# Position scores through memory in three transfers per tile, and the fourth tile's products earlier: one change to the last stage of a perceiver layer

## The chip, the core and the metric

The kernel runs on one core of a Trainium2 chip. The metric is the device time of one execution in microseconds (us), the median of several runs. The kernel before takes 3286.47 us (three runs, 3283.05 to 3294.87).

## The reference

Two layers work on x, 8 batches of 64 tokens with 512 features. The first has a cross attention over a context of 1601 rows, a Fourier attention and an expert layer. The second has a cross attention, a self attention with relative positions, and a quantized feed-forward layer. Only the last two blocks matter here:

```python
# _L1_attn_ref: 16 heads of 32, S = 64
r = _sinusoid_rel_pos(S, dk)
term1 = einsum('bhqd,bhkd->bhqk', Q, K)
term2 = einsum('bhqd,kd->bhqk', Q, r)
term3 = einsum('hd,bhkd->bhk', u, K)[:, :, None, :]
term4 = einsum('hd,kd->hk', v, r)[None, :, None, :]
scores = (term1 + term3 + _rel_shift(term2 + term4)) / sqrt(dk)
out = einsum('bhqk,bhkd->bqhd', softmax(scores), V).reshape(B, S, H * dv) @ Wo + bo
```

`_rel_shift` puts a column of zeros ahead of the 64 columns of each row, reads the 64 x 65 numbers as 65 x 64, and drops the first 64. The feed-forward layer rounds its weights to -1, 0 and 1 and its activations to 8 bits, and applies a gelu between its two products.

## The kernel before

`l1_tail` (from L1633) computes these two blocks. The 512 tokens are four tiles of 128, each with two batches (b). Tiles 0 to 2 form the group `first` and tile 3 the group `last`, because tile 3's x is completed last by the cross attention ahead of this stage. TensorE (PE) does the products, VectorE (DVE) and ScalarE (ACT) take results out of PSUM and do the softmax, GpSimd (POOL) adds biases, raises to the power of minus a half and clears borders, and SyncE (SP) issues all transfers, in the order in which they are written.

For a group, `turn` (L1694) transposes the normalized x into `xT`, `queries` (L1709) multiplies by Wq and makes two copies of the result for each tile: `qu` (with u added, by VectorE, L1722) and `qv` (with v added, by ScalarE, L1717). `of_pairs` (L1728) multiplies such a copy with a right side, per chunk c of 128 features, batch b and half j: 16 products of 64 rows by 64 columns in two passes each, into two PSUM banks. It serves the position scores (right side r, `y_ps`) and the scores (right side the keys, `s_ps`).

`positions_of` (L1747) does the relative shift. It copies the position scores of a tile into `y` (two buffers) with a zero column in front of each row, 65 numbers per row, and writes them to `shift[t]` in memory, in four transfers (two batches b, two heads h of a pair). `shifted` (L1770) reads them back one row (64 numbers) later, as rows of 64, into `z[t]` (three buffers), again in four transfers; a read can only be issued when its write has landed. A row of 65 numbers is a segment of 260 B and a row of 64 one of 256 B: per tile 2048 of each.

Each transfer uses one of eight semaphores in turn, and waits on SP until the transfer eight before it has landed. The order on SP is: Wq and small constants, Wk, Wv, Wo, the writes of tiles 0, 1 and 2 (12), the reads of tiles 0, 1 and 2 (12), `bo`, w1 (4), w2 (4), `b1`, `b2`, then the four writes and four reads of tile 3 and the four outputs.

Then come `keys` (kT, L1796), `values` (v, and x plus `bo` on GpSimd, L1806), and for each tile `probabilities` (L1808: s_ps plus z into `p`, then maximum, difference, exp, sum, reciprocal and product, L1815 to L1824), `turn` (transposes of p, L1833, copies by ScalarE, L1834), `attend` (o_ps, L1846, two halves weighted into `oT`, L1855 and L1856) and `out` (times Wo, L1864, added to x, L1871). `hidden` (L1883) normalizes and rounds a row, transposes it (`levels_ps`, L1877), multiplies by w1 (`h_ps`, L1902), adds b1 (L1906) and applies gelu and squares (L1907, L1909); `hidden_levels` rounds again, and `layer2` transposes the result, multiplies by w2 (L1930) and writes the output.

PSUM is held in three pools: `pe` (three banks, tag "e": y_ps, q_ps, xt_ps, h_ps), `pm` (three banks, tag "mm": k_ps, s_ps, v_ps, pT_ps, o_ps, out_ps) and `pt` (two banks: levels_ps).

The program is written in the order of the last lines of `l1_tail`, and a scheduler then orders the instructions of each engine; each engine works through its own queue in that order. In the built program VectorE's two copies of `v_ps` stand ahead of `p` of tile 0, and PE's queue has, after the scores of tile 0, the v products, the transposes and q products of tile 3 between them, then pT, o and out of tile 0, the scores of tile 1, the rest of q and y of tile 3, pT and o of tile 1, the levels of tile 0, out of tile 1, k and v of tile 3, the h products of tile 0 and the scores of tile 2.

Of the kernel before, what the change touches and what calls it, by code (L numbers as in the profile page):

```python
# [10 lines left out]
F32 = mybir.dt.float32  # L11
# [8 lines left out]
P = 128  # L20
B, S, D = 8, 64, 512
NT = B * S // P
DC = D // P
# [928 lines left out]
class Experts:  # L952
# [22 lines left out]
    def load(self, e):  # L975
        if e >= E_:
            return
        nc, d = self.K.nc, self.d
        w1, w2 = [], []
        for n in range(4):  # L980
            t = self.place(4 * e + n, "w1")
            nc.sync.dma_start(t, d["L0f_W1"][e, :, ts(n, 512)].rearrange("(c p) n -> p c n", p=P))
            w1.append(t)
        for n in range(4):
            t = self.pool.tile([P, DC, 512], F32, tag="w2", name="w2")
            nc.sync.dma_start(t, d["L0f_W2"][e, ts(n, 512), :].rearrange("(c p) n -> p c n", p=P))
            w2.append(t)
        self.held[e] = w1, w2
# [565 lines left out]
class TernaryWeights:  # L1554
# [46 lines left out]
        nc.vector.tensor_scalar(q, q, 1.0, -1.0, ALU.min, ALU.max)  # L1601
        nc.sync.dma_start(self.to[i], self.shaped(q, i))

    def load(self, pool):
        nc = self.nc
        self.w1 = pool.tile([P, DC, HID], BF16, tag="w1q", name="w1q")
        self.w2 = pool.tile([P, HID // P, D], BF16, tag="w2q", name="w2q")
        for c in range(4):
            nc.sync.dma_start(self.w1[:, c, :], self.w1_out[:, c, :])
        for c in range(4):  # L1610
            nc.sync.dma_start(self.w2[:, ts(c, 4), :], self.w2_out[:, ts(c, 4), :])


def rms_levels(K, pool, y, top, mean_square):
# [18 lines left out]
def l1_tail(K, x, d, w, known):  # L1633
# [6 lines left out]
    tc, nc = K.tc, K.nc  # L1640
    FIRST = NT - 1
    with ExitStack() as es:
        ep = es.enter_context(tc.tile_pool(name="e_e", bufs=1))
        wp = es.enter_context(tc.tile_pool(name="e_w", bufs=1))
        rp = es.enter_context(tc.tile_pool(name="e_r", bufs=2))
        dp = es.enter_context(tc.tile_pool(name="e_d", bufs=1, space=DRAM))
        pe = es.enter_context(tc.tile_pool(name="e_pse", bufs=3, space=PSUM))
        pm = es.enter_context(tc.tile_pool(name="e_psm", bufs=3, space=PSUM))
        pt = es.enter_context(tc.tile_pool(name="e_pst", bufs=2, space=PSUM))

        def big(name):
            return ep.tile([P, HID], F32, tag="big", name=name, bufs=3)
# [22 lines left out]
        uv = weight(ep, "L1a_uv", [P, 2, DC], d["L1a_uv"])  # L1675
        own = weight(ep, "c_own", [P, 4], d["c_own"])
        rT = weight(ep, "c_rT", [P, S], d["c_rT"])
        shift = [
            dp.tile([2, 2, DC, 2, S * (S + 1)], F32, tag=f"shift{t}", name="shift") for t in range(NT)
        ]  # L1680
        vs = ep.tile([P, DC, 2], F32, tag="vs", name="vs")
        for s in range(2):
            nc.vector.tensor_scalar_mul(vs[:, :, s], uv[:, 1, :], own[:, s : s + 1])
# [1 line left out]
        class Group:  # L1685
# [61 lines left out]
        def positions_of(t, qv):  # L1747
            y = ep.tile([P, 2, DC, 2, S + 1], F32, tag="y", name="y", bufs=2)
            halves = of_pairs(pe, "e", qv, lambda r, c, b: rT[r], "y_ps")
            nc.gpsimd.memset(y[:, :, :, :, 0:1], 0.0)  # L1750
            for j in range(2):
                K.copy(y[:, j, :, :, 1:], halves[j])
            for b in range(2):
                for h in range(2):
                    nc.sync.dma_start(
                        shift[t][b, :, :, h, :].rearrange("j c (q k) -> q (j c) k", k=S + 1),
                        y[ds(64 * h, 64), :, :, b, :].rearrange("q j c k -> q (j c) k"),
                    )

        first = Group(ep, list(range(FIRST)))  # L1760
        first.turn()
        first.queries()
        for t in first.tiles:
            positions_of(t, first.qv[t])
        wk = chunked(big("L1a_Wk"), "L1a_Wk")
        wv = chunked(big("L1a_Wv"), "L1a_Wv")

        z = {}

        def shifted(t):  # L1770
            z[t] = wp.tile([P, 2, 2, DC, S], F32, tag="z", name="z", bufs=3)
            for b in range(2):
                for h in range(2):
                    nc.sync.dma_start(
                        z[t][ds(64 * h, 64), b].rearrange("q j c k -> q (j c) k"),
                        shift[t][b, :, :, h, S:].rearrange("j c (q k) -> q (j c) k", k=S),
                    )

        for t in range(FIRST):
            shifted(t)  # L1780
        wo = chunked(wp.tile([P, HID], F32, tag="L1a_Wo", name="L1a_Wo"), "L1a_Wo")
        bo = weight(wp, "L1a_bo", [P, D], bcast_rows(d["L1a_bo"]))
        w.load(wp)
        b1 = weight(wp, "b1", [P, HID], bcast_rows(d["L1f_b1"]))
        b2 = weight(wp, "b2", [P, D], bcast_rows(d["L1f_b2"]))

        groups = [first]
        kT = wp.tile([P, DC, B * S], F32, tag="kT", name="kT")
        v = wp.tile([P, NT, D], F32, tag="v", name="v")

        def keys(g):
            n = len(g.tiles) * P
            for c in range(DC):
                ps = pm.tile([P, D], F32, tag="mm", name="k_ps")[:, :n]
                g.project(wk, c, ps)
                nc.scalar.copy(kT[:, c, ds(g.tiles[0] * P, n)], ps)  # L1796

        def values(g):
            for i, t in enumerate(g.tiles):
                ps = pm.tile([P, D], F32, tag="mm", name="v_ps")  # L1800
                for c in range(DC):
                    nc.tensor.matmul(
                        ps, lhsT=g.xT[:, c, ts(i, P)], rhs=wv[:, c, :], start=c == 0, stop=c == DC - 1
                    )
                K.copy(v[:, t, :], ps)
                nc.gpsimd.tensor_add(x[:, t, :], x[:, t, :], bo)  # L1806

        def probabilities(t):  # L1808

            zt = z[t].rearrange("p b j c k -> p j c b k")  # L1810
            p = ring("j", "p")
            qu = groups[t // FIRST].qu[:, :, t % FIRST]
            halves = of_pairs(pm, "mm", qu, lambda r, c, b: kT[r, c, ds((2 * t + b) * S, S)], "s_ps")
            for j in range(2):
                nc.vector.tensor_add(p[:, j], halves[j], zt[:, j])  # L1815
            rows = p.rearrange("p j c b k -> p (j c b) k")
            m = rp.tile([P, 16], F32, tag="m", name="m")
            wide = m.unsqueeze(2).to_broadcast([P, 16, S])
            nc.vector.tensor_reduce(m, rows, AX.X, ALU.max)
            nc.vector.tensor_sub(rows, rows, wide)  # L1820
            nc.scalar.activation(rows, rows, AF.Exp)
            nc.vector.tensor_reduce(m, rows, AX.X, ALU.add)
            nc.vector.reciprocal(m, m)
            nc.vector.tensor_mul(rows, rows, wide)  # L1824
            return p
# [35 lines left out]
        def out(t, oT):  # L1861
            ps = pm.tile([P, D], F32, tag="mm", name="out_ps")
            for c in range(DC):
                nc.tensor.matmul(  # L1864
                    ps,
                    lhsT=oT[:, c].rearrange("p b q -> p (b q)"),
                    rhs=wo[:, c, :],
                    start=c == 0,
                    stop=c == DC - 1,
                )  # L1870
            nc.vector.tensor_add(x[:, t, :], x[:, t, :], ps)  # L1871
# [60 lines left out]
            nc.vector.scalar_tensor_tensor(o, ps, level, x[:, t, :], ALU.mult, ALU.add)  # L1932
            nc.sync.dma_start(d["out"][ts(t, P), :], o)

        keys(first)
        p = probabilities(0)
        values(first)
        out(0, attend(0, turn(p)))
        p = probabilities(1)
        last = Group(wp, [FIRST])  # L1940
        last.turn()
        last.queries()
        positions_of(FIRST, last.qv[0])
        groups.append(last)
        out(1, attend(1, turn(p)))
        keys(last)
        values(last)
        shifted(FIRST)
        got = None
        for t in range(NT):  # L1950
            h = hidden(t)
            if got:
                layer2(t - 1, *got)
            if t + 2 < NT:
                p = probabilities(t + 2)
            got = hidden_levels(*h)
            if t + 2 < NT:
                out(t + 2, attend(t + 2, turn(p)))
# [118 lines left out]
```

## Time and profile before

| what | us or share |
|---|---|
| median of three runs | 3286.47 |
| the profiled execution, as a whole | 3286.85 |
| its span, from the first instruction to the last | 3285.1 |
| PE, DVE, ACT, POOL busy | 97%, 53%, 26%, 31% |
| first y_ps product of this stage | 3111.4 |
| scores of tile 0 done (PE) | 3134.46 |
| p of tile 0 begins (DVE) | 3147.60 |
| pT of tiles 0, 1 and 2 begins (PE) | 3155.33, 3179.16, 3213.32 |

The page of a profile shows one execution. Its slices cut the span into 40 equal parts, a digit being the busy share in tenths. The chain of work that ended last is followed back from the last instruction, at each step to what released it. A table by stage gives the busy time of each engine in stretches of the span, with the granted TensorE clock (1.00 is full, 0.50 half) and the mean busy share of the 16 DMA engines; groups that run into a stretch can make the share more than 1. In the timeline a line gives the start, the length, the engine, the source line, what is written from what, the count, and in brackets the idle time ahead of it with what ended it.

### The profile page before, as it was taken

The numbers are of one execution on the slowest core, as the hardware profiler recorded it, in microseconds if no ns is written. First come the engines' busy times: TensorE is split into PE (matmuls) and PEld (weight loads), VectorE is DVE, ScalarE is ACT, GpSimd is POOL, SyncE is SP. The second block draws the span as 40 slices with busy tenths as digits, with TensorE's granted clock in tenths as the row PEclk, the third lists the DMA queues.
The fourth block names the chain that finished last, engine by engine and source line by source line (L and its number), as shares of the span: only waits on it lengthen the run. The fifth ranks groups of instructions, "written<-read, shape, count | busy, mean of one in ns | idle before, by whom it ended". The sixth has DMA issues, their size and how long they took to land.

```text
span 3285.1 us, 40503 instructions
## 1 busy us (share of the span) xinstructions
PE 3174.3 (97%) x15881; PEld 2162.1 (66%) x15881; DVE 1749.7 (53%) x2929; ACT 846.4 (26%) x1572; POOL 1008.8 (31%) x980
## 2 busy tenths in 40 slices
PE   8999999999999999998899998999999999999986
PEld 6777778888878888885454444555565555655653
DVE  4745565666566656654332234644546455454736
ACT  2222232222233212211012221323233232323323
POOL 5433335444454435430000034123141321403010
PEclk9999999999999999998899998999999999999988
DMA  7254553333355333326278530100101001000250
GB/s 234 77 167 141 162 174 93 105 105 111 108 180 170 103 117 96 105 93 218 72 284 297 200 126 10 31 31 10 41 1 40 20 22 40 1 31 1 60 115 13
DMA packets 314322, 329.03 MB, mean 100 GB/s; under 512 B 35525, under 2 KB 235717, under 8 KB 312981
## 3 DMA queue, kind: packets, MB, share of 16 engines
q1 hardware_dynamic: 310416, 314.88, 30.6%
q10 hardware_dynamic: 3717, 11.57, 0.9%
q8 instruction: 126, 2.06, 0.3%
q14 instruction: 63, 0.52, 0.0%
HBM read 303.30 MB, written 23.10 MB: 99 GB/s over the span
## 4 chain that ended last, share of the span: by engine, by line
PE 89%; DVE 4%; DMA 3%; ACT 1%; issue 1%; POOL 1%; ACTq 0%; SPq 0%; POOLq 0%; DVEq 0%
PE k_ps L1298 11%; PE v_ps L1397 11%; PE x_ps L566 10%; PE x_ps L451 9%; PE z_ps L566 5%; PE s_ps L1411 4%; PE z_ps L451 4%; PE h_ps L1118 3%; PE oe_ps L1145 3%; PE acc L1461 3%; PE y_ps L566 2%; PE y_ps L451 2%; PE sum_ps L1320 2%; PE s_ps L444 1%; DMA w_out<-wq 1%; PE v_ps L599 1%
## 5 line engine op out<-in xcount | busy, mean ns | idle before, releaser
L1335 POOL TENSOR_TENSOR r<-r,minus_half 128x24 f32<-128x24 f32 x64 | 288.7, 4515 | 690.5 <-DVE r L1331 690.5
L1397 PE MATMUL v_ps<-L1x_WvT,ctxT 128*128 128x512 f32 (+1 forms) x832 | 380.2, 605 | 0.0
L1298 PE MATMUL k_ps<-ctxT,L1x_WkT 128*128 128x384 f32 (+1 forms) x1024 | 375.0, 509 | 0.6 <-ACT o L51 0.6
L451 PE MATMUL x_ps<-qt,ctxT 128*128 128x256 f32 x1152 | 286.6, 382 | 5.8 <-DVE s L416 3.8
L566 PE MATMUL x_ps<-pt,ctx 128*128 128x256 f32 x1152 | 280.3, 381 | 1.7 <-ACT u L514 1.0
L1298 PEld LDWEIGHTS k_ps<-ctxT,L1x_WkT 128*128 128x128 f32 x1024 | 183.9, 189 | 140.2 <-issue 42.8
L1397 PEld LDWEIGHTS v_ps<-L1x_WvT,ctxT 128*128 128x128 f32 (+1 forms) x832 | 149.6, 187 | 170.5 <-issue 165.1
L451 PEld LDWEIGHTS x_ps<-qt,ctxT 128*128 128x128 f32 x1152 | 217.2, 190 | 46.2 <-DVE s L416 7.3
L566 PEld LDWEIGHTS x_ps<-pt,ctx 128*128 128x128 f32 x1152 | 216.5, 189 | 35.3 <-DVE a L541 1.6
L122 POOL TENSOR_TENSOR ctxT<-ctxT 128x256 f32<-128x256 f32 x96 | 78.9, 822 | 405.8 <-DMA ctxT<-in_ctxT 355.6
L1411 PEld LDWEIGHTS s_ps<-qb,kT 64*128 64x128 f32 x1664 | 144.3, 187 | 75.4 <-DVE s L1423 44.5
L432 DVE TENSOR_TENSOR m<-m,s 128x512 f32<-128x512 f32 x176 | 131.3, 746 | 94.5 <-ACT s L430 91.8
L1411 PE MATMUL s_ps<-qb,kT 64*128 64x128 f32 x1664 | 171.5, 288 | 7.1 <-DVE s L1423 6.7
L122 POOL TENSOR_TENSOR ctx<-ctx 128x256 f32<-128x256 f32 x96 | 72.2, 752 | 341.4 <-DMA ctx<-in_ctx 276.8
L1302 ACT ACTIVATE kT<-k_ps,L1x_bk 128x384 f32<-128x384 f32 (+1 forms) x128 | 75.9, 593 | 349.5 <-PE k_ps L1298 344.1
L1331 DVE TENSOR_SCALAR r<-sumT_ps 128x12 f32<-128x12 f32 (+1 forms) x128 | 16.5, 166 | 254.5 <-PE sumT_ps L1328 254.1
L1400 ACT COPY v<-v_ps 128x512 f32<-128x512 f32 (+1 forms) x104 | 60.5, 582 | 336.8 <-PE v_ps L1397 336.8
L1423 DVE TENSOR_TENSOR s<-s_ps,r 128x512 f32<-128x512 f32 x192 | 124.6, 683 | 34.4 <-PE s_ps L1411 34.1
L484 DVE TENSOR_TENSOR s<-s,top_ps 128x1024 f32<-128x1024 f32 (+1 forms) x112 | 123.3, 1137 | 20.7 <-PE top_ps L474 20.7
L1452 DVE TENSOR_TENSOR s<-s,top_ps 128x1664 f32<-128x1664 f32 x64 | 117.9, 1884 | 27.1 <-PE top_ps L1448 27.1
L1431 DVE TENSOR_TENSOR fold<-s 128x1536 f32<-128x1536 f32 x64 | 112.1, 1751 | 37.7 <-ACT s L1453 37.7
L416 DVE SCALAR_TENSOR_TENSOR s<-y_ps,bias,p 128x256 f32<-128x256 f32 x96 | 46.3, 483 | 142.8 <-PE y_ps L451 142.7
(405 smaller groups left out, 5776.0 us busy)
## 6 DMA issues: line engine op xcount, KB each, us to landing
w<-in_L0f_W SPq DMA_DIRECT2D x64, 1024.0 KB, 5.4
ctxT<-in_ctxT SPq DMA_DIRECT2D x192, 256.0 KB, 4.4
ctx<-in_ctx SPq DMA_DIRECT2D x192, 256.0 KB, 3.2
ctxT<-in_ctxT SPq DMA_DIRECT2D x24, 768.0 KB, 4.4
wvT<-in_L0x_WvT SPq DMA_DIRECT2D x16, 1024.0 KB, 6.8
qk<-qk_all SPq DMA_DIRECT2D x15, 1024.0 KB, 7.1
qk_all<-stage SPq DMA_DIRECT2D x32, 384.0 KB, 3.5
wraw<-in_L1f_w1T SPq DMA_DIRECT2D x16, 512.0 KB, 4.2
```

Of the source, the lines that this page charges most:

```text
L122: nc.gpsimd.tensor_add(q[:, 4, :], q[:, 2, :], q[:, 3, :])
L432: nc.vector.tensor_max(self.m, self.m if k else self.s[:, LAST, :], self.s[:, k, :])
L451: nc.tensor.matmul(ps, lhsT=ctxT[i][:, Quarters.LEFT[n], ts(e, P)], rhs=right[n][:, e, :], start=start and e == 0, stop=e == 1, skip_group ...
L484: nc.vector.tensor_sub(s[:, k : k + n], s[:, k : k + n], top.unsqueeze(1).to_broadcast([P, n, HALF]))
L566: nc.tensor.matmul(ps, lhsT=ctx[pair][:, Quarters.LEFT[n], ts(m, P)], rhs=right[n][:, i, :], start=start and i == 0, stop=i == 2, skip_gro ...
L1298: nc.tensor.matmul(ps[:, :n], lhsT=wk[:, e, ts(c, P)], rhs=ctxT[i][:, e, :n], start=e == 0, stop=e == DC - 1)
L1335: nc.gpsimd.tensor_tensor(r[:, at : at + n, :], r[:, at : at + n, :], minus_half[:, :n, :], ALU.pow)
L1397: nc.tensor.matmul(ps[:kn], lhsT=ctxT[i][:, c, ds(at, kn)], rhs=wv[:, c, :], start=c == 0, stop=c == DC - 1)
L1411: nc.tensor.matmul(pair[j][:, i, :], lhsT=kT[c][rows, ts(k0 + i, P)], rhs=qb[rows, c, b].rearrange("p h q -> p (h q)"), start=True, stop=True,
L1423: nc.vector.tensor_mul(out, in_, by)
L1431: nc.vector.tensor_tensor(t, s[:, :, 0:6, :], s[:, :, 6:12, :], op)
L1452: nc.vector.tensor_sub(s[:, j], s[:, j], ps[:, j, :].unsqueeze(1).to_broadcast([P, NK, P]))
```

## The change

A tile's position scores now go to memory in one transfer from all 128 partitions, and come back in two (one for each half of 64 partitions), since `y`, `shift` and `z` have the two batches next to each other in memory. The transfers are put in another order on SP: write 0, `bo`, write 1, read 0, write 2, w1, read 1, `b1`, read 2, w2, `b2`. `load` is cut into `load1` and `load2` for that. `keys` and `values` of tile 3 use the banks "e" in place of "mm" and are written before its `positions_of`; `attend` and `out` of tile 1 move behind `hidden(0)`. Lines of the changed kernel are up to four lower than those quoted here.

```diff
-    def load(self, pool):
+    def load1(self, pool):
+    def load2(self, pool):
...
-        shift = [
-            dp.tile([2, 2, DC, 2, S * (S + 1)], F32, tag=f"shift{t}", name="shift") for t in range(NT)
-        ]
+        shift = [dp.tile([16, P * (S + 1)], F32, tag=f"shift{t}", name="shift") for t in range(NT)]
...
-            for b in range(2):
-                for h in range(2):
-                    nc.sync.dma_start(
-                        shift[t][b, :, :, h, :].rearrange("j c (q k) -> q (j c) k", k=S + 1),
-                        y[ds(64 * h, 64), :, :, b, :].rearrange("q j c k -> q (j c) k"),
-                    )
+            nc.sync.dma_start(
+                shift[t].rearrange("g (p k) -> p g k", k=S + 1), y.rearrange("p j c b k -> p (j c b) k")
+            )
...
-        for t in first.tiles:
-            positions_of(t, first.qv[t])
+        def shifted(t):
+            z[t] = wp.tile([P, 2, DC, 2, S], F32, tag="z", name="z", bufs=3)
+            for h in range(2):
+                nc.sync.dma_start(
+                    z[t][ds(64 * h, 64)].rearrange("q j c b k -> q (j c b) k"),
+                    shift[t][:, ds(h * S * (S + 1) + S, S * S)].rearrange("g (q k) -> q g k", k=S),
+                )
+
+        positions_of(0, first.qv[0])
         wk = chunked(big("L1a_Wk"), "L1a_Wk")
         wv = chunked(big("L1a_Wv"), "L1a_Wv")
...
-        for t in range(FIRST):
-            shifted(t)
         wo = chunked(wp.tile([P, HID], F32, tag="L1a_Wo", name="L1a_Wo"), "L1a_Wo")
         bo = weight(wp, "L1a_bo", [P, D], bcast_rows(d["L1a_bo"]))
-        w.load(wp)
+        positions_of(1, first.qv[1])
+        shifted(0)
+        positions_of(2, first.qv[2])
+        w.load1(wp)
+        shifted(1)
         b1 = weight(wp, "b1", [P, HID], bcast_rows(d["L1f_b1"]))
+        shifted(2)
+        w.load2(wp)
         b2 = weight(wp, "b2", [P, D], bcast_rows(d["L1f_b2"]))
...
-        keys(first)
+        keys(first, pm, "mm")
         p = probabilities(0)
-        values(first)
+        values(first, pm, "mm")
         out(0, attend(0, turn(p)))
         p = probabilities(1)
         last = Group(wp, [FIRST])
         last.turn()
         last.queries()
+        keys(last, pe, "e")
+        values(last, pe, "e")
         positions_of(FIRST, last.qv[0])
         groups.append(last)
-        out(1, attend(1, turn(p)))
-        keys(last)
-        values(last)
-        shifted(FIRST)
         got = None
         for t in range(NT):
             h = hidden(t)
-            if got:
+            if t == 0:
+                out(1, attend(1, turn(p)))
+                shifted(FIRST)
+            else:
                 layer2(t - 1, *got)
```

More of the change, by code (lines that the diff above doesn't have):

```diff
@@ L1602, in round @@
         nc.sync.dma_start(self.to[i], self.shaped(q, i))
-    def load(self, pool):
-        nc = self.nc
+    def load1(self, pool):
         self.w1 = pool.tile([P, DC, HID], BF16, tag="w1q", name="w1q")
+        for c in range(4):
+            self.nc.sync.dma_start(self.w1[:, c, :], self.w1_out[:, c, :])
+    def load2(self, pool):
         self.w2 = pool.tile([P, HID // P, D], BF16, tag="w2q", name="w2q")
         for c in range(4):
-            nc.sync.dma_start(self.w1[:, c, :], self.w1_out[:, c, :])
-        for c in range(4):
-            nc.sync.dma_start(self.w2[:, ts(c, 4), :], self.w2_out[:, ts(c, 4), :])
+            self.nc.sync.dma_start(self.w2[:, ts(c, 4), :], self.w2_out[:, ts(c, 4), :])
 def rms_levels(K, pool, y, top, mean_square):
@@ L1762, in l1_tail @@
         first.queries()
-        for t in first.tiles:
-            positions_of(t, first.qv[t])
+        z = {}
+        def shifted(t):
[6 more added lines that the diff above has]
+        positions_of(0, first.qv[0])
         wk = chunked(big("L1a_Wk"), "L1a_Wk")
         wv = chunked(big("L1a_Wv"), "L1a_Wv")
[L1768 to L1777, printed above, removed]
-        for t in range(FIRST):
-            shifted(t)
         wo = chunked(wp.tile([P, HID], F32, tag="L1a_Wo", name="L1a_Wo"), "L1a_Wo")
         bo = weight(wp, "L1a_bo", [P, D], bcast_rows(d["L1a_bo"]))
-        w.load(wp)
+        positions_of(1, first.qv[1])
[3 more added lines that the diff above has]
+        shifted(1)
         b1 = weight(wp, "b1", [P, HID], bcast_rows(d["L1f_b1"]))
+        shifted(2)
+        w.load2(wp)
         b2 = weight(wp, "b2", [P, D], bcast_rows(d["L1f_b2"]))
@@ L1789, in l1_tail, with keys, values @@
         v = wp.tile([P, NT, D], F32, tag="v", name="v")
-        def keys(g):
+        def keys(g, psum, tag):
             n = len(g.tiles) * P
             for c in range(DC):
-                ps = pm.tile([P, D], F32, tag="mm", name="k_ps")[:, :n]
+                ps = psum.tile([P, D], F32, tag=tag, name="k_ps")[:, :n]
                 g.project(wk, c, ps)
                 nc.scalar.copy(kT[:, c, ds(g.tiles[0] * P, n)], ps)
-        def values(g):
+        def values(g, psum, tag):
             for i, t in enumerate(g.tiles):
-                ps = pm.tile([P, D], F32, tag="mm", name="v_ps")
+                ps = psum.tile([P, D], F32, tag=tag, name="v_ps")
                 for c in range(DC):
@@ L1808, in probabilities @@
         def probabilities(t):
-            zt = z[t].rearrange("p b j c k -> p j c b k")
             p = ring("j", "p")
@@ L1814, in probabilities @@
             for j in range(2):
-                nc.vector.tensor_add(p[:, j], halves[j], zt[:, j])
+                nc.vector.tensor_add(p[:, j], halves[j], z[t][:, j])
             rows = p.rearrange("p j c b k -> p (j c b) k")
```

## The prediction

> **What bounds the kernel now.** I read the page first, for the whole program. TensorE (PE) is busy 97% of the span, and its row of slices shows dips only around 1480 to 1640 us, ahead of the experts, and at the end. The diff touches nothing ahead of `l1_tail`, whose products begin at 3111 us of 3285, so 174 us are in question.
>
> ```profile
> PE 3174.3 (97%) x15881; PEld 2162.1 (66%) x15881; DVE 1749.7 (53%) x2929; ACT 846.4 (26%) x1572; POOL 1008.8 (31%) x980
> PE   8999999999999999998899998999999999999986
> ```
>
> Second, the table by stage (stretch and its length, then busy us of PE, PEld, DVE, ACT and POOL, granted clock, DMA share, GB/s), cut where the granted clock changes:
>
> ```profile
> 3113.30:3116.70 3.40, 3.40 (x45) 3.40 (x43) 1.92 (x4) 1.12 (x2) 0.56 (x1) 1.00 0.97 324
> 3116.70:3123.50 6.80, 6.80 (x29) 5.44 (x29) 0.00 (x0) 0.05 (x1) 0.00 (x0) 0.50 1.36 118
> 3123.50:3147.40 23.90, 23.55 (x102) 13.45 (x101) 1.79 (x3) 3.58 (x7) 2.33 (x4) 1.00 1.00 155
> 3147.40:3150.80 3.40, 1.34 (x12) 1.15 (x11) 3.33 (x5) 0.00 (x0) 2.87 (x3) 1.00 1.03 392
> 3150.80:3164.50 13.70, 7.64 (x44) 4.94 (x45) 4.16 (x6) 5.16 (x11) 0.00 (x0) 0.50 0.57 221
> 3171.30:3185.00 13.70, 12.97 (x84) 11.17 (x84) 10.12 (x25) 4.56 (x9) 1.78 (x2) 0.50 0.26 40
> 3202.00:3205.40 3.40, 0.00 (x0) 0.00 (x0) 3.40 (x9) 2.21 (x5) 0.00 (x0) 1.00 0.00 0
> 3205.40:3215.70 10.30, 3.70 (x18) 2.84 (x19) 7.29 (x21) 2.89 (x4) 1.10 (x2) 0.50 0.00 2
> ```
>
> Until 3147 PE is full; then it stands still twice (3147 to 3155, 3202 to 3212), and behind each gap the clock is half. Third, the chain of work that ended last, from start, us, what:
>
> ```profile
> 3134.46 3.64 PE v_ps L1802 x8
> ...
> 3143.47 3.50 PE v_ps L1802 x8
> 3146.97 0.02 issue
> 3146.99 0.04 DVE v L49
> ...
> 3147.60 1.29 DVE p L1815 x2
> ...
> 3155.33 1.98 PE pT_ps L1833 x8
> ...
> 3161.42 5.21 PE out_ps L1864 x8
> 3166.63 1.98 PE s_ps L1738 x32
> ```
>
> The scores of tile 0 (`s_ps`) are done at 3134.46, but VectorE takes them up at 3147.60: its in-order queue has the copies of `v_ps` ahead of that softmax, and these wait for PE. When PE has run out of products the softmax takes 7.73 us with nothing beside it. Fourth, why it was queued so late, from the timeline (start, us):
>
> ```profile
> 3114.21 16.86 SPq L1755 DMA_DIRECT2D shift<-y  x12
> 3131.12 9.89 SPq L1774 DMA_DIRECT2D z<-shift  x12
> 3123.64 0.13 POOL L1750 MEMSET y<- 128x16 f32 x1 [9.59 <-DMA shift<-y]
> ```
>
> All twelve writes go ahead of the first read-back; z of tile 0 is complete at 3139 (fourth read issued 3133.2, 6 us to land).
>
> **The change, part by part.** The built order of the changed kernel is: k, s(0), the three v without a break, turn p(0), attend(0), out(0), s(1), then q, k, v and y of tile 3, hidden(0), attend(1), out(1), s(2). VectorE's queue now has softmax(0) ahead of two of the copies of v.
>
> *Transfers.* Bytes and segments are the same (2048 of 260 B written and 2048 of 256 B read per tile); four instructions become one, and eight semaphore lanes are no longer used up. No instruction of 2048 segments stands in the trace. Bounds: quarters of 512 landed 1.2 us apart (4.9 us a tile), while tile 0, behind the 1 MB of Wo, took 9.4 us from issue (3114.21) to the reuse of its y buffer (3123.64). I take 4.9 us, since the same 16 queues serve the same segments in both. Then tile 0's write lands at 3123.4 as now, its read waits behind `bo` (0.7) and tile 1's write (4.9) and two reads (2.7, the quarters being 0.67 apart): z(0) at about 3132, before s(0) ends. The softmax then runs 3134.6 to 3142.4, inside v (until 3144.8): 2.4 us of cover on VectorE, 2.5 on the transfer. ACT's copy of tile 2's y now stands ahead of the four copies of k and waits for the same write (3123.4); the first k product ends at 3124, and a fourth needs its bank at 3129, so it is free until the write is 5 us late. What is queued on SP behind waiting reads has room: w1q lands near 3141 (needed 3171), z(1) 3144 (3155), b1 3147 (3172), z(2) 3149 (3190), w2q 3155 (3208), z(3) 3186 (3216).
>
> *PE's path*, from 3134.46 to the start of pT of tile 2, which is now 3213.32:
> - three v at 3.44 (the row of tile 3's v): 10.3, to 3144.8.
> - pT(0) 1.0 (7 level transposes took 0.93 at full clock), the copy 0.6, o 1.1 (28 products 1.02 at full clock), oT 1.4, and 0.6 for a q product that waits for ACT behind oT: 4.7, to 3149.5. Now it is 6.1 at half clock.
> - out(0) 3.43 and s(1) 1.98: to 3154.9. Now 5.21 and 1.98.
> - q of tile 3: 30 passes of 0.111 (3.57 for k's 32) are 3.3, and 2.0 of wait: the fourth chunk needs the bank of the first, whose second `qu` stands on VectorE behind p 1.3, m 1.1, qu 0.3 and p 1.1. To 3160.2.
> - k 3.57 and 0.6 for a bank, v 3.44, y 2.0 (as s, same shape): to 3169.8. Softmax(1) and the levels of tile 0 take VectorE to about 3166 below this: 3.8 us of cover.
> - levels, 7 of pT(1), ACT's xT: 1.5, to 3171.3.
> - hidden(0) to out(1): 11.5. PE needs 3.5 for h, but the second copy of pT(1) stands on ACT behind gelu and squares (5.9 from the first bias op to the last square, 3197.04 to 3202.9 now), and oT on VectorE behind the levels of h(0). This wait is new, about 4 us of idle PE, then o at half clock. To 3182.8.
> - out(1) at half clock 5.2, s(2) 2.0: to 3190.0.
> - softmax(2) beside the levels of tile 1: now 11.75 (3201.57 to 3213.32), less the four maxima of h(0) (2.4), which are done before out(1): 9.3. To 3199.3.
>
> So 3213.3 becomes 3199.3: **14.0 us gained**. Behind it both orders are nearly the same, and I leave the 71.8 us to the end as they are.
>
> *The clock.* A stretch of 3.4 us with PE busy 1.34 (3147.4) or 0.00 (3202.0) is followed by 0.50. But 3113.3, busy 3.40 of 3.40 with `y_ps` alone (64 rows by 64 columns), is followed by 0.50 too. I go by the rows: dense 128-row products keep the clock, y, s and gaps lose it. Hence full clock up to 3174, half behind the gap after h(0) and behind s(2).
> The Trainium skill (TensorE: Matmul & The Clock Gate, "HAM oscillation") puts the drop down to PE idling longer than about 3.4 us. For the gaps the trace agrees; the row at 3113.3 was busy and dropped all the same. By that rule the y of tile 3 would cost no clock, and the sum would come out the same.
>
> **How this stands to the runs.** The profiled execution took 3286.85 us, 1.75 around its span of 3285.1, and 0.38 above the median of 3286.47. With 14.0 off: 3272.85 against the profiled one, **3272.5** against the median.
>
> **Rivals.**
> 1. *The clock stays up* behind the two remaining gaps: out(1) 3.4 for 5.2, and half of the 3.7 us of PE work now in 3205.4 to 3215.7, together 3.6; the three later stretches at 0.50 (from 3236.2, 3260.1 and 3273.7, with 4.75, 3.26 and 2.91 us of PE work) hold 5.5 more. Between 3.6 and 9.1 I take 6: 20 gained, 3266.5. Against it: 0.00 busy at 3202.0 was followed by 0.50. For it: the new gap has 4 us, so no 3.4 us of it need be as empty as those two. Chance 0.14.
> 2. *The clock drops early*: q's bank wait, y and s thin out 3150 to 3171, and it runs at half over 13.7 us as 3150.8 does now. That costs 6.9: 7 gained, 3279.5. For it: 3171.3 to 3185 stayed at 0.50 though PE was busy 12.97 of 13.70, with y in it. Against it: out(0) and the three products of tile 3 are 128-row work. Chance 0.18.
> 3. *The whole-tile transfer is slow*, and the kernel slower. Its place is SP's wait for all 2048 segments before the first read, with two writes ahead of z(0). If a write takes W instead of 4.9, z(0) comes 2(W - 4.9) later; up to W = 7.4 nothing waits, then each us costs two. The gain is gone at W = 14.4; at 22.6 it is 0.5% slower, 3303 (14.0 and 16.4 by two us each). For it: no such instruction in the trace. Against it: twelve small ones kept the queues at a DMA share of 1.00, so the number of instructions is not the limit. Chance 0.05 beyond 22.6, and 0.05 for 8 to 20 us late (3277 to 3302). The row of 9.4 as an upper bound gives 4 us, inside the forecast's own range.
> The Trainium skill (Perfetto Trace Analysis, "DMA Optimizations") says that splitting a transfer may let part of the work start sooner; a read of a quarter could then go 3.6 us before the whole write has landed. That speaks against joining; in the trace the reads of tile 3 did start so (3183.41, with later quarters in flight), but those of tiles 0 to 2 did not.
>
> **How the numbers follow.** The forecast (10 to 18 gained, 3268.5 to 3276.5) has 0.58. 0.5%, about what a measurement of this kernel can tell from no change, is 16.4 us: below 3270.0. Faster by more: 0.14 of rival 1 and 0.13 of the forecast's lower part, 0.27. Slower by more: 0.05. Within: 0.68. Eight in ten is from 3264 (rival 1 with 2.5 of margin) to 3282 (rival 2 with as much).
>
> **What would show it.** Right: `p` of tile 0 starts within 0.5 us of the end of s(0); the `v_ps` groups follow each other; PE has no gap at 3147 to 3155; the clock is 1.00 from 3150 to 3171; out(0) starts near 3149.5, pT(2) near 3199; a PE gap of 4 us behind h(0). Wrong: a `p` that waits for the DMA of z, a `kT` copy that waits for `shift`, landing of `shift` over 12 us from issue, or half clock over the products of tile 3.

## The result, and the profile after

| | before | after |
|---|---|---|
| median of 15 runs each, us | 3286.47 | 3273.92 |
| lowest and highest run, us | 3282.15, 3294.87 | 3267.11, 3282.25 |
| the profiled execution (its span), us | 3286.85 (3285.1) | 3276.05 (3274.3) |

The ratio of after to before is 0.9961, with a 95% interval of 0.9954 to 0.9969: 0.4% faster, 12.6 us by the medians. The forecast was 14.0 off, at 3272.5.

On the page after, TensorE is as busy as before, and the row of slices has the same dips: forty slices of 82 us are too coarse for this change.

```profile
PE 3169.4 (97%) x15875; PEld 2155.1 (66%) x15881; DVE 1755.5 (54%) x2929; ACT 847.6 (26%) x1572; POOL 1011.3 (31%) x980
PE   8999999999999999998899998999999999999986
```

The chain of work of after, from start, us, what:

```profile
3133.20 1.93 PE s_ps L1737 x32
3135.13 10.50 PE v_ps L1799 x24
3145.62 0.45 PE pT_ps L1829 x4
...
3150.20 3.44 PE out_ps L1860 x8
3153.64 1.98 PE s_ps L1737 x32
...
3183.28 6.54 PE out_ps L1860 x8
3189.82 1.98 PE s_ps L1737 x32
```

The three v products are one piece of 10.50 us where before had two breaks, and pT of tile 0 follows at once: the softmax and its 6.60 us of idle TensorE are off the chain. The timeline of after shows why (start, us; SP's queue, then VectorE's):

```profile
3114.90 0.37 SPq L1752 DMA_DIRECT2D shift<-y  x1
3124.43 2.54 SPq L1764 DMA_DIRECT2D z<-shift  x2
3135.16 1.29 DVE L1811 TENSOR_TENSOR p<-s_ps,z 128x512 f32<-128x512 f32 x2 [9.97 <-PE s_ps L1737]
```

The read of tile 0 is issued at 3124.43, as soon as its own write has landed (before: at 3131.12, behind all twelve writes), and all of z(0) has landed at 3132.30. What `p` waits for is the scores, no longer a copy of v and not the transfer. The table by stage, cut where the granted clock changes (stretch and length, busy us of PE, PEld, DVE, ACT and POOL, clock, DMA share, GB/s):

```profile
3117.36:3124.18 6.82, 6.82 (x29) 5.46 (x29) 0.00 (x0) 0.08 (x1) 0.00 (x0) 0.50 1.21 115
3124.18:3178.80 54.62, 48.67 (x303) 30.57 (x302) 28.12 (x50) 19.87 (x41) 7.55 (x9) 1.00 0.76 158
3178.80:3189.04 10.24, 7.73 (x35) 4.09 (x36) 3.62 (x14) 2.88 (x6) 0.55 (x1) 0.50 0.30 53
...
3195.86:3202.69 6.83, 3.48 (x14) 2.74 (x16) 5.12 (x13) 1.74 (x2) 1.75 (x2) 0.50 0.00 0
```

Full clock now holds for 54.6 us, through out(0), s(1) and the products of tile 3. It drops behind the wait that follows h(0), in which out(1) falls (6.54 us), and again behind s(2).

For what follows, one measure is used besides the ratios. In different executions the stage starts up to 6 us earlier or later (first y_ps at 3108 to 3114), which no edit here can cause. So each trace is cut at four marks and counted from the end of s(0) (the scores of tile 0; pT(2) are the transposes of tile 2, and so on): end of s(1), end of s(2), start of pT(2), end of the kernel. "Sum" is the whole way from s(0) to the end. The last column adds the time behind s(0) with the clock at 0.50.

| kernel | to s(1) | to s(2) | to pT(2) | to the end | sum | clock 0.50 |
|---|---|---|---|---|---|---|
| before | 34.1 | 33.0 | 11.6 | 71.9 | 150.6 | 52.3 |
| after | 20.4 | 36.2 | 10.3 | 72.2 | 139.1 | 34.1 |
| transfers_only | 20.4 | 33.6 | 11.6 | 70.4 | 136.0 | 30.7 |
| order_only | 34.2 | 34.2 | 10.3 | 74.4 | 153.0 | 51.3 |
| split_new_order | 25.0 | 36.6 | 10.3 | 74.5 | 146.3 | 41.0 |
| joined_old_order | 23.0 | 34.9 | 10.3 | 74.2 | 142.3 | 37.5 |
| late_z1 | 22.9 | 34.9 | 10.3 | 74.3 | 142.4 | 37.5 |
| early_out1 | 20.4 | 27.1 | 12.2 | 70.4 | 130.1 | 20.9 |
| no_b2 | 20.4 | 36.2 | 10.0 | 69.9 | 136.5 | 31.4 |
| fill_gaps | 20.4 | 33.3 | 13.0 | 72.7 | 139.5 | 23.9 |
| after_b2v | 20.4 | 36.2 | 10.3 | 72.0 | 138.9 | 34.1 |
| transfers_b2v | 20.4 | 34.8 | 11.6 | 73.8 | 140.6 | 45.1 |
| early_b2v | 20.4 | 27.1 | 12.2 | 70.3 | 130.0 | 20.7 |
| kv_mm | 20.4 | 33.1 | 10.3 | 71.4 | 135.2 | 30.7 |

The first column repeats to a tenth wherever the engines' queues are the same. Three pairs differ in nothing but one addition of tile 3 and show how far one execution can be trusted behind that: transfers_only and transfers_b2v have 136.0 and 140.6, but early_out1 and early_b2v 130.1 and 130.0, after and after_b2v 139.1 and 138.9.

Of the 11.5 us between the two sums, 13.7 are gained before s(1) ends, 3.2 are lost from there to s(2), 1.3 come back before pT(2), and 0.3 are lost behind it. The theory to be tested (A below) is that the transfers earn everything, by an earlier z(0); the rival (B), that the moved products do.

### The profile page after: what moved, and what is told of

Same layout as the page of the kernel before. It is cut to its first block, busy times and chain, and to the rows that moved or that the text cites. A ratio compares the mean times of both kernels' runs of the same rounds, so it can differ in the third digit from the quotient of the medians.

```text
span 3274.3 us, 40479 instructions
## 1 busy us (share of the span) xinstructions
PE 3169.4 (97%) x15875; PEld 2155.1 (66%) x15881; DVE 1755.5 (54%) x2929; ACT 847.6 (26%) x1572; POOL 1011.3 (31%) x980
## 3 DMA queue, kind: packets, MB, share of 16 engines
q1 hardware_dynamic: 310096, 314.88, 30.7%
## 4 chain that ended last, share of the span: by engine, by line
PE 90%; DVE 4%; DMA 3%; ACT 1%; issue 1%; POOL 1%; SPq 0%; ACTq 0%; POOLq 0%; DVEq 0%
PE k_ps L1298 11%; PE v_ps L1397 11%; PE x_ps L566 10%; PE x_ps L451 9%; PE z_ps L566 5%; PE s_ps L1411 4%; PE z_ps L451 4%; PE h_ps L1118 3%; PE oe_ps L1145 3%; PE acc L1461 3%; PE y_ps L566 2%; PE y_ps L451 2%; PE sum_ps L1320 2%; PE s_ps L444 2%; PE qk_ps L237 1%; PE v_ps L599 1%
## 5 line engine op out<-in xcount | busy, mean ns | idle before, releaser
L122 POOL TENSOR_TENSOR ctx<-ctx 128x256 f32<-128x256 f32 x96 | 72.7, 757 | 342.5 <-DMA ctx<-in_ctx 271.6
L1423 DVE TENSOR_TENSOR s<-s_ps,r 128x512 f32<-128x512 f32 x192 | 124.7, 683 | 34.3 <-PE s_ps L1411 34.1
L1452 DVE TENSOR_TENSOR s<-s,top_ps 128x1664 f32<-128x1664 f32 x64 | 117.9, 1884 | 27.1 <-PE top_ps L1448 27.1
```

The costliest lines, as they stand in the source:

```text
L122: nc.gpsimd.tensor_add(q[:, 4, :], q[:, 2, :], q[:, 3, :])
L1423: nc.vector.tensor_mul(out, in_, by)
L1452: nc.vector.tensor_sub(s[:, j], s[:, j], ps[:, j, :].unsqueeze(1).to_broadcast([P, NK, P]))
```

## The experiments

### Which half of the change earns it

**transfers_only** takes the changed kernel and puts the products back:

```diff
-        keys(last, pe, "e")
-        values(last, pe, "e")
         positions_of(FIRST, last.qv[0])
...
+        out(1, attend(1, turn(p)))
+        keys(last, pm, "mm")
+        values(last, pm, "mm")
...
```

> The changed transfers (one write and two reads per tile, the new order on SP), with the products in the order of the kernel before: y of tile 3 right behind q, attend and out of tile 1 ahead of hidden(0), k and v of tile 3 behind out(1) and in the banks 'mm'. Theory A (the gain is the cover of softmax(0): z early enough that VectorE takes p of tile 0 up at the end of s(0)): p(0) starts within 0.5 us of the end of s(0), no gap of TensorE between v and pT(0), and 10 to 14 us below the kernel before, so nearly all of the gain. Theory B (the gain is the fourth tile's products in the waits of tile 1): at most 5 us below the kernel before.

Measured: ratio 0.9951 (0.9934 to 0.9967), median 3271.69. z(0) lands 3.5 us ahead of the end of s(0), p(0) starts 0.03 us behind it, and the first column is that of after, 20.4. Theory A holds: this half alone gives the whole gain.

**order_only** has the transfers of before and the products of after.

> The changed order of the products, with the transfers of the kernel before (four writes and four reads per tile, all twelve writes ahead of the reads). Theory A: z of tile 0 still lands near 3139, VectorE's copies of v stay ahead of p(0), so TensorE stands still from 3147 to 3155 as before; what is moved only fills the wait behind s(1) and gives it back behind h(0): within 3 us of the kernel before. Theory B: 9 to 14 us below it.

Measured: ratio 1.0010 (0.9997 to 1.0022), median 3290.26 against 3285.84: no gain; whether there is a small loss stays open, since the interval reaches across 1. z(0) lands 4.1 us behind the end of s(0), but VectorE takes p(0) up only 13.1 us behind it, as late as before, after the second copy of v (timeline of order_only):

```profile
3147.09 1.28 DVE L1815 TENSOR_TENSOR p<-s_ps,z 128x512 f32<-128x512 f32 x2
```

TensorE stands still for 6.67 us ahead of pT(0), at half clock behind it. Theory B falls. Of the 13.1 us by which p(0) is late, then, 9.0 pass with z(0) already there.

### Joining the transfers, or their order on SP

**split_new_order** is the changed kernel with four writes and four reads per tile (and the layout of `shift` and `z` that goes with them), in the new order on SP.

```diff
-            nc.sync.dma_start(shift[t].rearrange(...), y.rearrange(...))
+            for b in range(2):
+                for h in range(2):
+                    nc.sync.dma_start(shift[t][b, :, :, h, :]..., y[ds(64 * h, 64), :, :, b, :]...)
...
```

> As the changed kernel in its order of products and its order on SP, but with four writes and four reads per tile in place of one and two. Theory A (the order counts, not the number of instructions): the same 2048 segments in the same order, so z(0) lands within 2 us of 3132; one copy of v stands ahead of p(0) in VectorE's queue, so p(0) starts about 3.5 us later than in the changed kernel, and the kernel is 4 to 8 us slower than the changed one, 5 to 9 us faster than before. Theory C (joining the transfers is what makes them fast: 0.64 us of issue each, and lanes that wait): z(0) lands at 3137 or later, SP's queue runs late to the end, and at most 3 us of the gain are left.

Measured: ratio 0.9981 (0.9971 to 0.9991), median 6.6 us below before. z(0) lands 1.2 us ahead of the end of s(0), against 2.8 in after: with the new order alone it is still in time. Yet pT(0) comes 4.7 us later than in after, and by the ratios half of the gain is lost. VectorE's timeline shows two copies of v in the way, each waiting for a product:

```profile
3134.24 0.69 DVE L49 COPY v<-v_ps 128x512 f32<-128x512 f32 x1 [12.65 <-PE v_ps L1805]
...
3142.16 0.69 DVE L49 COPY v<-v_ps 128x512 f32<-128x512 f32 x1 [3.52 <-PE v_ps L1805]
```

The first stands ahead of p(0), which so starts 4.3 us behind s(0). The second stands inside softmax(0), and a copy on ScalarE stands ahead of its exp: the softmax takes 10.7 us in place of 7.7. In after it ended 2.6 us before pT(0), so 4.7 of these 7.3 us are lost. So theory A holds for the transfer, and the loss comes from the places of copies of 0.6 to 0.7 us each in the queues. Those places are the scheduler's choice, and the number of transfers, with their layout, is all that differs ahead of it; joining pays by way of the queue. No run shows why the scheduler chooses so.

The Trainium skill (Perfetto Trace Analysis, "DMA Optimizations") says that splitting may let part of the work start sooner. Here the first split read was issued 12.2 us ahead of the end of s(0), the joined one 10.7; but z was complete 1.6 us later.

**joined_old_order** joins them, but keeps SP's old order: three writes, six reads, then bo and the weights.

> As the changed kernel, joined transfers included, but SP in the old order: the three writes, then the six reads, then bo, w1, w2, b1, b2. z(0) has one write more ahead of it (4.9 us) and lands near 3136 in place of 3132, some 1 us after s(0) ends at 3135. Theory A: p(0) waits 1 to 2 us for z, which the 2.4 us of cover on VectorE take up: 0 to 3 us slower than the changed kernel. Theory D (the new order on SP is what counts, joined or not): 8 us or more slower than the changed kernel.

Measured: ratio 0.9967 (0.9954 to 0.9980). z(0) lands 1.0 us behind the end of s(0), and here `p` does wait for it (timeline):

```profile
3134.16 1.29 DVE L1809 TENSOR_TENSOR p<-s_ps,z 128x512 f32<-128x512 f32 x2 [12.16 <-DMA z<-shift]
```

It starts 1.1 us behind s(0), pT(0) comes 2.3 us later than in after, and the kernel is 3.2 us longer than after by the sums. Theory D falls: by the sums about three quarters of the gain survive the old order.

Four kernels have the products of after and differ in the transfers alone. Joining brings z(0) forward by 3.1 us in the old order (from 4.1 behind s(0) to 1.0 behind) and by 1.6 in the new one; the new order brings it forward by 5.3 us with split transfers and by 3.8 with joined ones. So the order does more for the landing. For the time it is the other way round: the kernel with neither has a ratio to before of 1.0010, that with the new order alone 0.9981, with joining alone 0.9967, with both 0.9961.

**late_z1** writes tile 0 twice, the first time to a spare place, to price a late z(0), as rival 3 of the prediction has it.

> As the changed kernel, but the write of tile 0 is made twice, first to a spare place in memory that nothing reads, so 2048 more segments of 260 B stand ahead of z(0). The forecast took 4.9 us for a write. Theory A: z(0) lands 4.9 us later, about 2 us behind the end of s(0) in place of 2.8 us ahead of it; the built program has one copy of v ahead of p(0), which holds p(0) back by 3.5 us anyway; pT(0) starts 14 to 16 us behind the end of s(0) in place of 10.4, and the kernel is 2 to 7 us slower than the changed one. Theory C (a whole-tile write costs 9 us of the path, as from its issue to its landing): z(0) lands 6 us or more behind the end of s(0), pT(0) starts 18 us or more behind it, and the whole gain is gone.

Measured: ratio 0.9978 (0.9967 to 0.9989), the sum 3.3 us above after. z(0) came 6.6 us later than in after, not 4.9: the two writes landed 6.8 us apart. p(0) starts 4.3 us behind s(0), and pT(0) comes 12.6 behind it, 2.3 us later than in after, where theory A had 14 to 16. Theory C falls. But the run does not price a late z(0) by itself: z(0) had landed at 3138.06, and p(0) starts at 3138.50, when a copy of v ahead of it is done that had waited for its product until 3137.89. With that queue an earlier z(0) would not have let p(0) start earlier.

### Where the moved products lose what they fill

**early_out1** keeps every product of tile 3 where the change put it and takes pT(1), o(1) and out(1) from behind h(0) into their midst:

```diff
         keys(last, pe, "e")
+        pT = turn(p)
         values(last, pe, "e")
+        oT = attend(1, pT)
         positions_of(FIRST, last.qv[0])
+        out(1, oT)
...
             if t == 0:
-                out(1, attend(1, turn(p)))
                 shifted(FIRST)
```

> As the changed kernel, but pT(1) stands behind k of tile 3, o(1) behind v, and out(1) behind y, all ahead of hidden(0). In the changed kernel TensorE stands still for 3.26 and 1.70 us behind h(0), and out(1) takes 6.54 us at the dropped clock. Theory E (this wait is what the moved products cost): the gap is gone, out(1) takes about 3.44 us, the scores of tile 2 end some 6 to 10 us earlier against the end of s(0), and the kernel is 4 to 8 us faster than the changed one. Theory F (VectorE and ScalarE set the time of this stretch, since softmax(2) and the levels of tiles 0 and 1 must pass them anyway): within 2 us of the changed kernel.

Measured: ratio 0.9951 (0.9932 to 0.9970), the sum 9.0 us below after. The gap is gone. The timeline of early_b2v, whose queue of TensorE is the same, shows it:

```profile
3167.70 1.04 PE L1829 MATMUL pT_ps<-ident,p 128*128 128x128 f32 x8
3168.57 3.60 PE L1799 MATMUL v_ps<-L1a_Wv,xT 128*128 128x512 f32 x8
3172.10 1.10 PE L1842 MATMUL o_ps<-pT,v 64*64 64x128 f32 x32
3173.13 2.00 PE L1737 MATMUL y_ps<-c_rT,qv 64*128 64x64 f32 x32
3175.06 3.70 PE L1860 MATMUL out_ps<-L1a_Wo,oT 128*128 128x512 f32 x8
```

Each line begins where the one above ends, and out(1) takes 3.70 us. s(2) ends 9.1 us earlier than in after (27.1 for 36.2). Of this, softmax(2) on VectorE takes 1.9 back (12.2 for 10.3), and the way behind it is 1.8 shorter (70.4 for 72.2), with less time at half clock. Theory E holds in the profile. By the ratios of the runs the difference to after is 3.3 us, and the two intervals overlap; early_b2v below tests it again.

**fill_gaps** leaves after's order and adds 42 products that nothing reads, to hold the clock:

```diff
             if t == 0:
+                fill(14)
                 out(1, attend(1, turn(p)))
...
                 p = probabilities(t + 2)
+                if t == 0:
+                    fill(28)
```

> As the changed kernel, with 42 products more (128 rows by 512 columns, about 0.216 us each, of w1 with itself; nothing reads the result) around h(0), pT(1), o(1) and behind s(2), where TensorE stands still in the changed kernel. Theory K (the clock is what these gaps cost): the clock stays at 1.00 over out(1) and over the levels of tile 1, out(1) takes 3.44 us in place of 6.54, pT(2) and the h products of tile 1 take half, and the kernel is 3 to 5 us faster than the changed one. Theory L: the products stand in TensorE's queue ahead of work that is ready, 9 us of them at full clock and 18 at half: the kernel is 1 to 6 us slower, though out(1) may be at full clock.

Measured: ratio 0.9963 (0.9951 to 0.9975), the same as after. The clock did stay up: out(1) took 3.70 us and s(2) ended 2.9 us earlier. But pT(2) hardly started earlier than in after (46.3 us behind s(1) for 46.5), as the timeline of fill_gaps shows (TensorE, then VectorE):

```profile
3194.31 4.47 PE L1898 MATMUL h_ps<-w1q,xT 128*128 128x512 bf16 x15
3198.61 1.04 PE L1829 MATMUL pT_ps<-ident,p 128*128 128x128 f32 x8
...
3196.90 1.22 DVE L1820 TENSOR_TENSOR p<-p,m 128x1024 f32<-128x1024 f32 x1
```

In this built order 15 of the h products of tile 1 stand ahead of pT(2) in TensorE's queue (in after it is 2), while softmax(2) is done at 3198.12. The clock fell at 3193.1, behind a wait of 3.99 us. Theory K holds for the clock up to s(2) and not for the total; the loss of theory L is not seen either. What that clock would be worth with the queue unchanged stays open.

**kv_mm** puts k and v of tile 3 into the banks "mm" again.

> As the changed kernel, but k and v of tile 3 use the banks 'mm', as before the change, in place of 'e'; the built order of TensorE is the same. In the changed kernel three chunks of q and then k, v and y of tile 3 share the three banks 'e', and q waits 1.90 us and k 0.35 us for one. Theory P (the banks are only a place): the waits for 'e' go or move to 'mm', where s(1) and pT(1) stand; within 2 us of the changed kernel. Theory Q (the banks 'e' were needed for the moved products): k waits for p(1) to free the scores' banks, and the kernel is 3 us or more slower than the changed one.

Measured: ratio 0.9956 (0.9944 to 0.9968), the sum 3.9 us below after. Theory Q falls, and the expectation was wrong in one thing: the built order of TensorE is not the same (timeline):

```profile
3151.53 2.72 PE L1704 MATMUL q_ps<-xT,L1a_Wq 128*128 128x128 f32 x22
3154.09 2.40 PE L1704 MATMUL k_ps<-xT,L1a_Wk 128*128 128x128 f32 x20
3156.32 1.06 PE L1704 MATMUL q_ps<-xT,L1a_Wq 128*128 128x128 f32 x8
3157.22 1.50 PE L1704 MATMUL k_ps<-xT,L1a_Wk 128*128 128x128 f32 x12
```

With other banks, products of k stand in the 1.90 us for which the fourth chunk of q waits for a bank "e". In after k needs a bank "e" itself and stands behind it. So the change's own choice of banks costs it 2.75 us up to out(1) (which starts 45.40 us behind s(0) against 48.15). In the runs this is no more than a hint: the intervals of the two ratios overlap (0.9956 and 0.9961).

### The last bias

**no_b2** leaves the four additions of b2 out.

> As the changed kernel, without GpSimd's four additions of b2 (the bias is left out of the output). In the changed kernel the one of tile 1 (3194.92 to 3196.68) stands ahead of the power that the levels of tile 1 wait for, and VectorE stands still from 3196.62 to 3197.64. Theory G: that wait is part of the 3 us by which pT(2) starts later than forecast; without it the levels of tile 1 begin about 1 us earlier, and the kernel is 1 to 2 us faster than the changed one. Theory H: VectorE makes the time up with softmax(2): within 0.5 us at pT(2).

Measured: ratio 0.9956 (0.9939 to 0.9973). pT(2) comes only 0.3 us earlier, since VectorE still waits 0.73 us for the power where it waited 1.02: theory H at that place. The sum is 2.6 us lower for another reason: at tile 3 the 1.19 us wait is gone, and the first h products behind it fall into full clock (four in 1.05 us, where eight took 3.47). The interval of the ratio overlaps that of after, so the runs settle neither theory for the total.

**after_b2v**, **transfers_b2v** and **early_b2v** are after, transfers_only and early_out1 with that one addition on VectorE, side by side on one chip:

```diff
-            nc.gpsimd.tensor_add(x[:, t, :], x[:, t, :], b2)
+            (nc.vector if t == NT - 1 else nc.gpsimd).tensor_add(x[:, t, :], x[:, t, :], b2)
```

> As the changed kernel, with b2 of tile 3 added by VectorE instead of GpSimd, nothing left out. In the changed kernel GpSimd's addition stands ahead of the power for the levels of tile 3, and VectorE stands still for 1.19 us. Without all four additions the stretch from the start of out(3) to the end was 34.6 us in place of 37.1. Theory G: the addition on VectorE (0.7 us) fits into the 0.6 us in which VectorE waits for the power anyway: that stretch takes 35 to 36.5 us, and the kernel is 0.5 to 2 us faster than the changed one. Theory H: the additions of tiles 0 to 2 are what mattered in the kernel without them: the stretch stays at 37 us.

Measured: ratio 0.9961 (0.9949 to 0.9973). The stretch from out(3) takes 36.8 us: 0.3 less, and theory G falls. The addition fits, but then the output of tile 2 (0.75 us) goes ahead of the levels in VectorE's queue.

> The changed transfers with the order of products of the kernel before, and b2 of tile 3 added by VectorE. Beside the kernel after_b2v it tells what the changed order of products brings by itself. In the profiles without that edit, from the end of s(0) to the end of the kernel, the transfers alone took 136.0 us and the whole change 139.1. Theory M (the moved products cost about 3 us, as the wait behind h(0) and the dropped clock over out(1) outweigh what they fill): 1 to 5 us faster than after_b2v. Theory N (the difference was one execution's clock): within 1 us of after_b2v.

Measured: ratio 0.9965 (0.9953 to 0.9976), median 3272.16, where after_b2v has 3272.22. Theory M falls and N holds: the 3.1 us between the profiles of transfers_only and after are within what one execution's clock does. The profile of transfers_b2v spent 45.1 us at half clock, that of transfers_only 30.7.

> The kernel early_out1 (pT(1), o(1) and out(1) inside the products of tile 3, ahead of hidden(0)) with b2 of tile 3 added by VectorE. In the profile without that edit it took 130.1 us from the end of s(0) to the end, the changed kernel 139.1 and the transfers alone 136.0; its runs were 16 us below the kernel before, those of the transfers alone 14. If the profile's order holds: 4 to 10 us faster than after_b2v, 2 to 7 faster than transfers_b2v, the fastest here, 17 to 21 us below the kernel before. If softmax(2) and the levels on VectorE are the bound in most executions: within 2 us of transfers_b2v.

Measured: ratio 0.9946 (0.9934 to 0.9958), median 3266.43: 19.4 us below before, 5.8 below after_b2v and 5.7 below transfers_b2v, the fastest kernel here. Its interval just overlaps that of after_b2v; the two profiles of this order, 9 us shorter than the two of after's, speak for a real difference.

## Why the prediction was right, point by point

- *Transfers and softmax(0).* z(0) forecast at about 3132 and measured at 3132.30 (2.5 and 2.8 us ahead of the end of s(0), which came 0.7 later); p(0) within 0.5 us of s(0), measured 0.03 (3135.16 and 3135.13). pT(0) 10.3 behind s(0), measured 10.33; out(0) 15.0 and 14.9; the end of s(1) 20.4 and 20.4. This is the whole of the gain (34.1 to 20.4). transfers_only and order_only show that the transfers bring it, and split_new_order that an early z(0) is not enough without the places of p(0) and of the copies of v in the queue. No run keeps the old transfers and puts p(0) ahead of those copies. An estimate from the rows of before: z(0) was there at 3139.14, so with 7.7 us of softmax pT(0) could have started 12.4 us behind s(0), where it started 20.9 behind in before and 10.3 in after. By that estimate the place in the queue is worth about 8.5 us and the earlier landing about 2; the prediction named both and did not tell them apart.
- *A write at 4.9 us* was a little small. With bo between them, write 1 landed 6.1 us behind write 0 (5.6 forecast), and late_z1 priced one more at 6.6. z(0) was on time because its reads were complete 1.8 us behind write 1, not 2.7: two errors that cancel, which is luck.
- *The sign "landing of `shift` over 12 us from issue"* came up, though the forecast held: write 1 took 12.6 us (3117.91 to 3130.47). Half of that was its wait behind write 0, which landed at about 3124.4, so a time from issue was the wrong sign.
- *The cover of 2.4 us on VectorE* is real: in after softmax(0) ends 2.6 us before pT(0) starts, and in late_z1 p(0) began 4.3 us late, the softmax took 0.5 longer, and pT(0) came 2.3 us late. But it belongs to one order of the queue. In joined_old_order p(0) began 1.1 us late, inside the cover, and pT(0) still lost 2.3: the softmax takes 11.5 us (3134.16 to 3145.63) in place of 7.7, of which a copy of v on VectorE takes 1.9, one on ScalarE ahead of the exp 1.0, and a slower last step 0.9 (2.12 for 1.22; no run shows why).
- *q's bank wait*, 2.0: measured 1.90. It was right as a term, but nothing made it necessary: kv_mm filled it with k.
- *The wait behind h(0)*, 11.5 us from the h products to out(1), with 4 us idle: 11.0 (3172.24 to 3183.28), with 3.26 and 1.70 idle. early_out1 shows that this was the price of putting attend(1) there.
- *out(1) at half clock*, 5.2: measured 6.54. The row it came from (out(0) of before, 3161.42 to 3166.63) lies across the end of a half-clock stretch at 3164.5, 3.1 us in it and 2.1 behind. It was a mixture. Twice the 3.44 of a full-clock one is the bound that should have been taken.
- *softmax(2) beside the levels*, 9.3: measured 10.3. GpSimd's b2 explains 0.3 of the 1.0 (no_b2); the rest is not settled.
- *The end*, 71.8 unchanged: 72.2. It is not a constant: 69.9 to 74.5 in the table, going with the half-clock stretches that fall into it.
- *Sum.* 14.0 forecast, 11.5 by the profiles' sums, 12.6 by the medians. The terms that were too small (1.3, 1.0 and 0.4, less 0.2 elsewhere) make up the 2.5.
- *Clock.* Full up to 3174 and half behind h(0) and s(2), as forecast. Rival 1 (it stays up) didn't happen by itself; fill_gaps forced it as far as s(2), for nothing in the total. Rival 2 (it drops over tile 3's products) didn't happen here, but does in transfers_only, and for 3.4 us in joined_old_order and late_z1 and 6.8 us in split_new_order, so after was not far from it. Rival 3 didn't happen, and its price stays open: by its working 5.0 us of a late z(0) are free, but in the runs with a later z(0) the queues differ too. Its "8 to 20 us late" does not follow from its own formula, by which 3277 to 3302 belong to a z(0) 9.5 to 34.5 us late.

What the prediction did not say is that the change's second half earns nothing (order_only 1.0010, and transfers_b2v and after_b2v within 0.1 us of each other). Its own terms held it: from s(1) to s(2) they add up to 35.1 us, where before took 33.0.

## What to carry to other kernels

Add a ledger up by stage against the kernel before, not only in total: a part that only moves a wait shows itself there. When a late input holds up an in-order queue, the question is where the queue's builder puts its consumer, which can be worth more than the transfer itself. Take no duration from a row without the clock of its stretch beside it, and move work into a wait only when its own consumers don't end up behind the next stage.

## What the runs showed of the hardware

The clock did not go by the length of the idle time. In transfers_only and in after TensorE stands still for the same 1.9 us behind q. The first line is a stretch of transfers_only, after which the clock fell to 0.50; there y (64 rows by 64 columns) is 0.7 us of its work. The other two are stretches of after: behind the first, all in 128-row products, it stayed at 1.00, behind the second it fell.

```profile
3154.48:3157.90 3.42, 1.80 (x15) 1.71 (x15) 3.42 (x7) 2.26 (x5) 0.00 (x0) 1.00 0.00 0
```

```profile
3158.31:3161.72 3.41, 1.60 (x14) 1.63 (x15) 3.41 (x7) 2.25 (x5) 0.00 (x0) 1.00 0.02 8
...
3175.38:3178.80 3.42, 0.96 (x8) 0.34 (x5) 3.31 (x6) 3.42 (x10) 0.00 (x0) 1.00 0.25 18
```

The Trainium skill (TensorE: Matmul & The Clock Gate, "HAM oscillation") puts the drop down to idle gaps longer than about 3.4 us. Here it followed longest gaps of 1.89 and 3.26 us, so the trace does not agree. Nor does the trace of before bear it out for all of its gaps, as the prediction had it: the clock fell at 3171.3 in a gap of 3.16 us (3168.56 to 3171.72), and at 3150.8 some 2.1 us into a longer one. It looks as if the kind of product in a stretch of 3.4 us counts too. In 128-row products alone the stretch of transfers_only has 1.06 us; in joined_old_order one with 1.05 us of them and nothing else (3156.25 to 3159.66) was followed by 0.50 as well, where the 1.60 us in after kept the clock. That is inferred from these few stretches, not tested by itself.

A joined write of 2048 segments took 0.37 us on SP against four times 0.64; but a later instruction stood there for 2.4 to 4.9 us (w2 in after: 4.91). What it waited for there no view shows.
